# Part of du*B moved to TensorE, sums over states by transposes, convolutions on 32x32 tiles

## The chip, the cores and the metric

The kernel runs on one core of a Trainium2 chip. The metric is the device time of one execution in microseconds (us). The kernel before took 19,314.11 us (median of three runs, 19,313.31 to 19,316.24).

## The reference

Four layers follow one another on an image of 4 x 48 x 48 pixels with 192 channels, all in float32. Each of them contains selective scans over 2304 pixels (or, in the last layer, over rows of 48), with 16 states for each inner channel. The scan of the first layer, which the others share up to names:

```python
xz = u @ inW.T
xh, z = jnp.split(xz, 2, axis=-1)
xc = jax.nn.silu(_causal_conv(xh, cW, cB))
xdbl = xc @ xpW.T
dt = xdbl[..., :R]
Bm = xdbl[..., R:R + N]
Cm = xdbl[..., R + N:]
delta = jax.nn.softplus(dt @ dtW.T + dtB)
A = -jnp.exp(Alog)
def step(h, t):
    d_t, u_t, b_t, c_t = t
    h = jnp.exp(d_t[..., None] * A) * h + (d_t * u_t)[..., None] * b_t[:, None, :]
    return (h, jnp.sum(h * c_t[:, None, :], axis=-1))
...
y = jnp.swapaxes(ys, 0, 1) + xc * Dp
return y * jax.nn.silu(z) @ outW.T
```

The first layer runs four such blocks with 384 inner channels (along columns forward and backward, then along rows both ways, with a normalisation between) and a causal convolution of 3 taps. The second layer has a convolutional branch and four scan directions with 192 inner channels; the third has four scan directions without projections. The last layer runs four blocks with 384 inner channels and 4 taps on single rows and single columns (the state starts at zero in each), and then an MLP.

## The kernel before

**Jobs and groups.** The image is cut into six chunks of 384 pixels. A job is one chunk of one image in one scan direction; each of the four layers has 96 jobs. In the first and the last layer a job has 384 inner channels, as three blocks `i` of 128 partitions, and 16 states, as four groups `g` of NG = 4. So it has 12 groups. In the two layers between, the partitions hold two halves of the states of 64 channels (`parts = 2`), and a job has 6 groups. A group is a tile of 128 partitions by four states by 384 pixels (385 where the state is carried from chunk to chunk, with one column for the entering state).

**One group.** `decay` makes the four tiles exp(delta * A) on ScalarE, and with `i == 0` fetches B and C of the group's states, each row copied to all 128 partitions (`fetch`, one tile `bcb` of 2 x 4 x 384). `scan` does two VectorE instructions: the product of `du` (in PSUM) with B of the four states into the PSUM tile `inputs`, and one scan over the four states laid end to end. `weigh` multiplies h by C on GpSimd. `reduce` sums the four states on TensorE, each as a product with an identity, into the PSUM tile `y` of the block; `skip` puts D * x there first, by a diagonal matrix. When all four groups are in, `take` copies `y` to SBUF on ScalarE (`yt`) and `gate` multiplies it by silu(z) on GpSimd.

**One job.** `units` lists what a job needs before its groups: projections `inner`, depthwise convolutions `conv` (products with one diagonal 128x128 matrix per tap, then Silu on ScalarE), `bc` (B, C and the low-rank dt of the chunk, copied to SBUF as `bcd` and stored to DRAM as `bc`), `delta` (dt, Softplus), the gate's z, and the outputs of an earlier job. `drive` makes delta * x on GpSimd (`dus`), and `enter` copies it into the PSUM tile `du`. In the last layer a forward job and its backward twin share projections and z.

**The order.** `run_jobs` writes the order of every engine by hand, and TensorE, VectorE, GpSimd and ScalarE keep it. In turn t it issues: `scan` of group t; `decay` of group t + 2; `take` of a finished block; `weigh` of group t; then what the `Stream` of the next job's units has in this slot (0 to 11), its TensorE part before its ScalarE part, at most two units ahead, since the PSUM pool `ps` has two buffers; the side work of a normalisation, in some jobs; `gate` of an earlier block; `drive` of the block that begins at group t + 3; and `reduce` of group t - 1 (`behind` = 1). There are three buffers of decays, four of h in the last layer and three in the first, and five and four of `bcb`. All DMAs go through the queue of SyncE.

Of the kernel before, what the change touches and what calls it, by code (L numbers as in the profile page):

```python
# [14 lines left out]
ALU = mybir.AluOpType  # L15
# [11 lines left out]
NG = 4  # L27

# [30 lines left out]
class K:  # L59
# [3 lines left out]
    def __init__(self, tc, ctx):  # L63
        self.tc, self.nc = tc, tc.nc
        self.v, self.g, self.t = (
            InOrder(tc, e) for e in (tc.nc.vector, tc.nc.gpsimd, tc.nc.tensor)
        )
        self.count = 0
        self.last_act = None
        self.table = None  # L70
        self.const = ctx.enter_context(tc.tile_pool(name="const", bufs=1))
        self.ident = self.tile(self.const, [128, 128], "ident")
        make_identity(self.nc, self.ident)

# [163 lines left out]
class ScanPools:  # L238
# [6 lines left out]
    def __init__(self, k, ctx, parts, rows):  # L245
        pool = k.tc.tile_pool
        self.parts, self.rows = parts, rows
# [9 lines left out]
        self.y = ctx.enter_context(pool(name="y", bufs=2 if rows else 1, space=PSUM))  # L257
# [3 lines left out]
        inputs = k.tile(self.vec, [128, 1536 if rows else 2048], "inputs")  # L261
        self.b = inputs[:, : NG * W].rearrange("p (j l) -> p j l", l=W)
# [4 lines left out]
        self.n_decays = 0  # L267

# [40 lines left out]
class ScanJob:  # L309
# [12 lines left out]

    def __init__(self, k, pools, w, c0, rev, prev):
# [7 lines left out]
        self.du = {}  # L331

# [14 lines left out]
    def projections(self, xs, *slots):  # L347
# [5 lines left out]
        def bc(px):  # L353
# [4 lines left out]
            self.bc = k.dram([2 * N, W], "bc")  # L358
            nc.sync.dma_start(self.bc, self.bcd[: 2 * N, :])
# [21 lines left out]

    def fetch(self, g):
# [3 lines left out]
        self.bcb[g] = k.tile(pools.bcs, [128, 2, NG, pools.W], "bcb")  # L386
        self.fetched[g] = []
        for m in range(pools.parts):
            at = (m * pools.groups + g) * 2 * NG
            ins = k.nc.sync.dma_start(  # L390
                self.bcb[g][m * wide : (m + 1) * wide].rearrange("p s j l -> p (s j l)"),
                self.bc[at : at + 2 * NG, :].rearrange("r l -> (r l)").partition_broadcast(wide),
            )
            self.fetched[g].append(ins)

# [18 lines left out]
    def carry(self, i, g):  # L414

        if not self.pools.rows and self.prev is not None:
            at = self.entry
            ins = self.k.g.tensor_copy(
                self.bcb[g][:, 0, :, at : at + 1].squeeze(2),
                self.prev.state[:, i, g * NG : (g + 1) * NG],  # L420
# [8 lines left out]
    def enter(self, i):  # L429

        self.pools.turn(self.k, self.rev)
        self.pools.entered = self.k.copy(self.pools.du[:, self.tokens], self.du.pop(i))

    def scan(self, i, g):
# [6 lines left out]
        if pools.n_h >= pools.hbufs:  # L441
# [5 lines left out]
            b, du.unsqueeze(1).to_broadcast([128, NG, W]), self.bcb[g][:, 0, :, :], ALU.mult  # L447
# [3 lines left out]
        k.v.tensor_tensor_scan(  # L451
            h.rearrange("p j l -> p (j l)")[:, ::step],
            self.a.pop((i, g)).rearrange("p j l -> p (j l)")[:, ::step],
            b.rearrange("p j l -> p (j l)")[:, ::step],
            0.0,
            ALU.mult,
            ALU.add,
        )

    def weigh(self, i, g):  # L460
# [11 lines left out]
        ins = k.g.tensor_tensor(ht, ht, self.bcb[g][:, 1, :, self.tokens], ALU.mult)  # L472
        pools.weighed.append(ins)

    def reduce(self, i, g):
# [6 lines left out]
        h = self.h.pop((i, g))  # L482
        for j in range(NG):
# [63 lines left out]
class MambaJob(ScanJob):  # L547
# [50 lines left out]

    def units(self, last):
        k, w, two, halo = self.k, self.w, self.pools.two, self.w.taps - 1  # L600
# [13 lines left out]
        def conv(i, *slots):  # L614

            offs = [at + (halo - t) * (1 if self.rev else -1) for t in range(w.taps)]

            def act(ps):
                if i == 0:
                    self.xs = k.tile(two, [128, 3, CH], "xc")  # L620
                k.act(self.xs[:, i, :], ps, AF.Silu, bias=w.cb[:, i, :])

            return self.unit(
                slots,
                128,
                lambda ps: (
                    self.shaped(ps),
                    [(w.diag[:, i, t, :], self.part(i, off)) for t, off in enumerate(offs)],
                ),
                act,  # L630
            )
# [9 lines left out]
        if self.twin is not None:  # L641
# [3 lines left out]
            return [conv(0, 0, 0), conv(1, 1, 2), conv(2, 2, 2), bc, *deltas, *outputs]  # L645
# [6 lines left out]
            *(conv(i, min(2 + i, 3), 3) for i in range(3)),  # L652
# [10 lines left out]
    def skip(self, i):  # L663

        self.k.mmo(self.y[i], [(self.w.diagD[:, i, :], self.xs[:, i, :])], stop=False)

    def take(self, i):
        if i == 0:
            self.yt = self.k.tile(self.pools.one, [128, 3, CH], "yt", self.pools.yts)
        self.k.copy(self.yt[:, i, :], self.y[i])  # L670
# [115 lines left out]
def run_jobs(jobs, side=None):  # L786
# [4 lines left out]
    ahead, behind, taken, gated, driven = 2, 1, 2, 3, 3  # L791
# [20 lines left out]
    jobs[0].enter(0)  # L812
    for job, i, g in groups[:ahead]:
        job.decay(i, g)
    stream = Stream([])
    for t in range(len(groups) + gated + 1):
# [21 lines left out]
        if t < len(groups):  # L838
# [4 lines left out]
            job.weigh(i, g)  # L843
        stream.run(at if at < per - 1 else per)
        if t < len(groups):
# [12 lines left out]
        if 0 <= t - behind < len(groups):  # L858
            job, i, g = groups[t - behind]
            job.reduce(i, g)  # L860
    Stream(jobs[-1].outputs(*[(0, 0)] * 3)).run(per)
# [37 lines left out]
class MambaWeights(Weights):  # L899
    def __init__(self, k, pool, inT, xpT, dtT, vec, tag):  # L900
# [6 lines left out]
        self.diag = k.tile(pool, [128, 3, self.taps, 128], f"diag{tag}")  # L907

    def scaled(self, out, by):
        self.k.nc.vector.tensor_scalar(out, self.k.ident, by, None, ALU.mult)  # L910

    def diagonals(self, i):

        self.scaled(self.diagD[:, i, :], self.D[:, i, :])
        for t in range(self.taps):
            self.scaled(self.diag[:, i, t, :], self.vec[:, i, 19 + t : 20 + t])
# [13 lines left out]
class PairWeights(MambaWeights):  # L930
# [18 lines left out]
    def scaled(self, out, by):  # L949
        if not self.late:  # L950
            return super().scaled(out, by)
        self.k.act(out, self.k.ident, AF.Identity, scale=by)
# [933 lines left out]
```

## Time and profile before

| | |
|---|---|
| median of three runs | 19,314.11 us |
| profiled execution, its own time | 19,328.76 us |
| its span | 19,327.0 us |
| VectorE busy | 18,079.9 us (94%) |
| TensorE matmul busy, weight loads busy | 16,851.2 us (87%), 7,999.8 us (41%) |
| GpSimd busy | 14,748.4 us (76%) |
| ScalarE busy | 13,012.9 us (67%) |
| DMA, share of 16 engines | 41.1% |
| first layer, last layer | about 0 to 6,150 us, 12,836 to 18,890 us |

In the profile PE is TensorE, PEld its weight loads, DVE VectorE, ACT ScalarE, POOL GpSimd and SP SyncE. A group's line gives line, engine and operation, output and inputs by the names of the program's tiles, shapes, count, then the busy time in us and the mean of one in ns, then the engine's idle time before it with what ended it. Nearly all instructions have line 56, that of a helper which records the order, so they are told apart by tiles and shapes. A timeline's line gives start, length, engine, operation and count. A float32 product shows as two MATMULs with a weight load each.

### The profile page before, as it was taken

The numbers are of one execution on the slowest core, as the hardware profiler recorded it, in microseconds if no ns is written. First come the engines' busy times: TensorE is split into PE (matmuls) and PEld (weight loads), VectorE is DVE, ScalarE is ACT, GpSimd is POOL, SyncE is SP. The second block draws the span as 40 slices with busy tenths as digits, with TensorE's granted clock in tenths as the row PEclk, the third lists the DMA queues.
The fourth block names the chain that finished last, engine by engine and source line by source line (L and its number), as shares of the span: only waits on it lengthen the run. The fifth ranks groups of instructions, "written<-read, shape, count | busy, mean of one in ns | idle before, by whom it ended". The sixth has DMA issues, their size and how long they took to land.

```text
span 19327.0 us, 166155 instructions
## 1 busy us (share of the span) xinstructions
PE 16851.2 (87%) x49392; PEld 7999.8 (41%) x49392; DVE 18079.9 (94%) x7297; ACT 13012.9 (67%) x23158; POOL 14748.4 (76%) x10860
## 2 busy tenths in 40 slices
PE   8999999999998877787787778879999999999989
PEld 4544545444444322222222222234444444444444
DVE  9999999999998699999999999969999999999993
ACT  6766767666665467777777777766666666666663
POOL 7888888778886288888888888857777777777770
PEclk9999999999999878788887787889999999999999
DMA  3333333232332366666666666633322332333231
GB/s 114 118 112 115 122 110 127 104 117 106 117 117 90 91 142 141 151 149 152 151 150 146 141 151 148 140 110 110 107 106 104 107 112 105 109 110 112 103 107 47
DMA packets 500517, 2306.77 MB, mean 119 GB/s; under 512 B 76664, under 2 KB 334304, under 8 KB 347168
## 3 DMA queue, kind: packets, MB, share of 16 engines
q1 hardware_dynamic: 499616, 2296.14, 41.1%
q8 instruction: 396, 6.49, 0.1%
q14 instruction: 505, 4.14, 0.1%
HBM read 2103.60 MB, written 192.32 MB: 119 GB/s over the span
## 4 chain that ended last, share of the span: by engine, by line
DVE 47%; POOL 31%; PE 9%; issue 8%; ACT 3%; DMA 1%; POOLq 0%; SPq 0%; DVEq 0%; ACTq 0%
DVE h L56 30%; POOL h L56 24%; DVE inputs L56 16%; PE y L56 3%; PE ps L56 3%; POOL dus L56 2%; PE vps L128 2%; POOL state L56 1%; POOL yt L56 1%; ACT a L93 1%; PE mop L128 1%; POOL bcb L56 1%; PE mps L128 1%; DMA bcb<-bc 1%; POOL nx L56 1%
## 5 line engine op out<-in xcount | busy, mean ns | idle before, releaser
L56 POOL TENSOR_TENSOR h<-h,bcb 128x1536 f32<-128x1536 f32 x3456 | 11906.7, 3445 | 1599.4 <-DVE h L56 1137.0
L56 DVE TENSOR_TENSOR_SCAN h<-a,inputs 128x1540 f32<-128x1540 f32 (+1 forms) x3456 | 11606.4, 3358 | 145.0 <-DVE inputs L56 1.4
L93 ACT ACTIVATE a<-delta,A 128x384 f32<-128x384 f32 (+1 forms) x13824 | 7419.1, 602 | 2684.0 <-DVE h L56 2666.7
L56 PE MATMUL y<-h,ident 128*128 128x384 f32 x18432 | 6741.6, 514 | 440.9 <-POOL h L56 438.2
L56 DVE TENSOR_TENSOR inputs<-du,bcb 128x1540 f32<-128x1540 f32 (+1 forms) x3456 | 6112.5, 1769 | 419.0 <-ACT a L93 120.1
L56 PEld LDWEIGHTS y<-h,ident 128*128 128x128 f32 x18432 | 3614.9, 200 | 3410.5 <-POOL h L56 863.3
L56 PE MATMUL y<-h,sum 128*64 128x384 f32 x9216 | 2668.5, 643 | 746.0 <-POOL h L56 540.2
L56 POOL COPY state<-h 128x4 f32<-128x4 f32 x2304 | 431.5, 187 | 1950.4 <-DVE h L56 1912.0
L56 PEld LDWEIGHTS y<-h,sum 128*64 128x64 f32 x9216 | 853.6, 167 | 2175.2 <-issue 968.8
L56 PE MATMUL ps<-xh,diag 128*128 128x384 f32 x4032 | 1418.8, 491 | 171.2 <-ACT xc L93 171.0
L56 PE MATMUL ps<-bcd,dtT 12*128 12x384 f32 (+1 forms) x2304 | 1138.8, 608 | 453.0 <-ACT delta L93 449.7
L56 PE MATMUL ps<-u,inT 96*128 96x384 f32 x3456 | 1253.7, 493 | 162.2 <-ACT z L93 118.5
L56 PEld LDWEIGHTS ps<-xh,diag 128*128 128x128 f32 x4032 | 750.6, 189 | 765.9 <-ACT xc L93 259.3
L93 ACT ACT_TABLE_LOAD x794 | 1018.7, 1283 | 14.0
L90 ACT ACT_TABLE_LOAD x789 | 1012.3, 1283 | 14.2 <-PEq L1876 0.7
L56 PEld LDWEIGHTS ps<-u,inT 96*128 96x128 f32 x3456 | 650.0, 191 | 673.6 <-ACT z L93 194.8
L93 ACT ACTIVATE delta<-ps,vec 128x384 f32<-128x384 f32 x1152 | 632.2, 578 | 384.5 <-PE ps L56 379.1
L93 ACT ACTIVATE o<-ps 64x384 f32<-64x384 f32 (+1 forms) x864 | 409.2, 474 | 711.0 <-PE ps L56 711.0
L56 PEld LDWEIGHTS ps<-bcd,dtT 12*128 12x128 f32 (+1 forms) x2304 | 427.4, 213 | 1098.0 <-ACT delta L93 693.6
L56 PE MATMUL ps<-yt,outT 128*96 128x384 f32 x2304 | 789.8, 486 | 0.4 <-POOL yt L56 0.4
L93 ACT ACTIVATE du<-dus 128x384 f32<-128x384 f32 x1152 | 557.6, 484 | 141.1 <-DVE inputs L56 132.2
L56 PE MATMUL ps<-yc,sum 128*64 128x384 f32 x1152 | 643.6, 649 | 0.7 <-ACT yc L93 0.7
(133 smaller groups left out, 10570.8 us busy)
## 6 DMA issues: line engine op xcount, KB each, us to landing
bcb<-bc SPq DMA_DIRECT2D x384, 1540.0 KB
bcb<-bc SPq DMA_DIRECT2D x768, 770.0 KB
bcb<-bc SPq DMA_DIRECT2D x384, 1536.0 KB
y<-o SPq DMA_DIRECT2D x192, 288.0 KB
xs<-xi_wh SPq DMA_DIRECT2D x96, 288.0 KB
xs<-xi_hw SPq DMA_DIRECT2D x96, 288.0 KB
added<-y SPq DMA_DIRECT2D x96, 288.0 KB
xs<-x_wh SPq DMA_DIRECT2D x96, 288.0 KB
```

Source lines behind the costliest of these rows:

```text
L56: return lambda *a, **kw: self.tc.keep_in_program_order(op(*a, **kw))
L90: self.in_order(self.nc.scalar.preload_act_table_set(LOG_EXP))
L93: return self.in_order(self.nc.scalar.activation(out, in_, func, **kw))
L128: ins = (engine or self.nc.tensor).matmul(out, lhsT, rhs, start=start and i == 0, stop=stop and i == n - 1)
```

## The change

**du*B.** Of the four states of a group, VectorE keeps the product for `given` = 4 - `made`; TensorE makes the rest, `made` = 1 in the first layer, 2 in the last and none between. To have du on the contracted side, `turn` transposes `du` of a block on TensorE (three 128x128 transposes through `ps`, copied to SBUF by ScalarE as `duT`). B of a made state has to stand on the diagonal of a 128x128 matrix for each 128 pixels: `spread` stores these rows to DRAM as `be`, and copies them element by element from there onto the diagonals of images in DRAM that are zeroed once per layer (8 of them, two sets of four used in turn). `fetch` loads the diagonal matrices with a second DMA, into the same tile as B of the given states and C. `fill` then makes three products of 128 columns for each made state into the PSUM tile `fills`, which has one buffer. The scan of a group becomes two instructions, over the given states from `inputs` and over the made ones from `fills`; in the first layer the second scan starts from the carried state as its initial value.

**Sums.** With one part, `reduce` adds the four states to `y` by twelve 128x128 transposes that accumulate in PSUM, so `y` stands transposed (pixels on partitions). `skip` becomes three products with x as the stationary operand. `take` copies the transposed `y` to SBUF (`yT`), and the new `turn_back` transposes it back through `ps`, with another ScalarE copy to `yt`. `y` has one PSUM buffer in all layers (it had two in the last).

**Convolutions.** The diagonal matrices become strips of 32 columns. A unit makes two halves of 192 pixels, each by four 32x32 tiles per tap, so that eight products stand on eight different tiles; it holds both buffers of `ps`, and ScalarE applies Silu to each half. To make room for two halves at once, quarter r of a block goes to quarter (r + i) % 4; the weights are permuted on the host (`TURN`) to match.

**Order.** `behind` becomes 2 in the last layer; `take` and the gate follow it. All three convolution units of a forward job have slot 3. In turn t, `turn_back` comes before the stream, `turn` (for the block that begins at t + 2) after it, and `fill` of group t + 1 last, after `reduce`.

The core of the diff:

```diff
-        inputs = k.tile(self.vec, [128, 1536 if rows else 2048], "inputs")
-        self.b = inputs[:, : NG * W].rearrange("p (j l) -> p j l", l=W)
+        banks = -(-self.given * W // 512)
+        inputs = k.tile(self.vec, [128, banks * 512], "inputs")
+        self.b = inputs[:, : self.given * W].rearrange("p (j l) -> p j l", l=W)
+        self.fills = []
+        if made:
+            fills = k.tile(self.vec, [128, made * 512], "fills")
+            starts = (512 - CH, 512) if made == 2 else (0,)
+            self.fills = [fills[:, at : at + CH] for at in starts]
+            self.joined = fills[:, starts[0] : starts[0] + made * CH]
...
+            for n in range(2 * self.groups):
+                d = k.dram([128 * (self.line + 1)], "dg")
+                k.nc.sync.dma_start(d.rearrange("(t x) -> t x", x=self.line + 1), zeros)
+                self.diags.append(d)
...
+    def spread(self):
+        k, pools = self.k, self.pools
+        sync = k.nc.sync
+        n = N // NG * (pools.given + NG)
+        self.bc = k.dram([n, pools.W], "bc")
+        sync.dma_start(self.bc, self.bcd[:n, :])
+        if not pools.made:
+            return
+        be = k.dram([N // NG, pools.made, CH], "be")
+        sync.dma_start(be.rearrange("q e l -> (q e) l"), self.bcd[n : 2 * N, self.tokens])
...
+            for e in range(pools.made):
+                with k.nc.allow_non_contiguous_dma(reason="diagonal"):
+                    sync.dma_start(
+                        line[:, :, e, m, 0:1], be[q, e].rearrange("(b t v) -> t b v", t=128, v=1)
+                    )
...
+        if pools.made:
+            line = self.lines[g][: 128 * pools.line].rearrange("(t x) -> t x", t=128)
+            k.nc.sync.dma_start(t[:, n:], line)
...
+    def fill(self, i, g):
+        k, pools = self.k, self.pools
+        for b in range(3):
+            for e, out in enumerate(pools.fills):
+                for m in range(pools.parts):
+                    k.t.matmul(
+                        out[m * pools.wide : (m + 1) * pools.wide, b * 128 : (b + 1) * 128],
+                        self.duT[i][:, b, :],
+                        self.bcb[g][2][:, b, e, m, :],
+                        start=True,
+                        stop=True,
+                        skip_group_check=True,
+                    )
...
-            b, du.unsqueeze(1).to_broadcast([128, NG, W]), self.bcb[g][:, 0, :, :], ALU.mult
+            b, du.unsqueeze(1).to_broadcast([128, pools.given, W]), self.bcb[g][0], ALU.mult
...
+        n = pools.given
+        scan(flat(0, n), b.rearrange("p j l -> p (j l)"), 0.0)
+        if pools.made and pools.rows:
+            scan(flat(n, NG), pools.joined, 0.0)
+        elif pools.made:
+            for e, fill in enumerate(pools.fills):
+                j = g * NG + n + e
+                first = 0.0 if self.prev is None else self.prev.state[:, i, j : j + 1]
+                scan((v[:, n + e, self.tokens] for v in (h, a)), fill, first)
...
+        if parts == 1:
+            for j in range(NG):
+                ht = h[:, j, self.tokens]
+                for n in range(3):
+                    at = slice(n * 128, (n + 1) * 128)
+                    ins = k.t.matmul(
+                        self.y[i][:, at],
+                        ht[:, at],
+                        k.ident,
+                        start=False,
+                        stop=g == pools.groups - 1 and j == NG - 1,
+                        is_transpose=True,
+                        skip_group_check=True,
+                    )
+            pools.readers.append(ins)
+            return
...
+                for t, off in enumerate(offs):
+                    for r in range(4):
+                        at_r = slice(r * 32, (r + 1) * 32)
+                        for (i, n), ps in zip(both, made):
+                            c = (r + i) % 4
+                            k.t.matmul(
+                                self.shaped(ps[c * 32 : (c + 1) * 32]),
+                                w.diag[at_r, i, t, :],
+                                self.half(i, n, off)[at_r],
...
-            return [conv(0, 0, 0), conv(1, 1, 2), conv(2, 2, 2), bc, *deltas, *outputs]
+            return [conv(0, 0, 0), conv(1, 2, 2), conv(2, 2, 2), bc, *deltas, *outputs]
...
-            *(conv(i, min(2 + i, 3), 3) for i in range(3)),
+            *(conv(i, 3, 3) for i in range(3)),
...
     def take(self, i):
+        self.turned = self.k.tile(self.pools.one, [128, CH], "yT")
+        self.k.copy(self.turned, self.y.pop(i))
...
-    ahead, behind, taken, gated, driven = 2, 1, 2, 3, 3
+    behind = 2 if jobs[0].pools.rows else 1
+    ahead, taken, gated, driven = 2, behind + 1, behind + 2, 3
...
+        if back := at_group(t - gated, last_group):
+            back[0].turn_back(back[1])
         stream.run(at if at < per - 1 else per)
+        if soon := at_group(t + 2, 0):
+            soon[0].turn(soon[1])
...
             job.reduce(i, g)
+        if t + 1 < len(groups):
+            job, i, g = groups[t + 1]
+            job.fill(i, g)
```

## The prediction

> **What bounds the kernel now.** I read the page's busy line first, then the busy time by stage, the groups of instructions with shapes kept apart, and the timeline of single groups. The busy line and two long stretches, first the last layer (13,000 to 18,800 us), then the first (100 to 6,050 us):
>
> ```profile
> PE 16851.2 (87%) x49392; PEld 7999.8 (41%) x49392; DVE 18079.9 (94%) x7297; ACT 13012.9 (67%) x23158; POOL 14748.4 (76%) x10860
> 13000.00:18800.00 5800.00, 5316.37 (x15043) 2831.02 (x15042) 5703.64 (x2229) 3825.25 (x6591) 4449.57 (x2246) 0.95 0.30 108
> 100.00:6050.00 5950.00, 5540.20 (x15928) 2932.17 (x15928) 5731.22 (x2235) 4106.88 (x7222) 4897.10 (x4079) 0.97 0.32 114
> ```
>
> The columns of the stretches are length, busy PE, PEld, DVE, ACT, POOL, granted clock, DMA share, GB/s. DVE is 98% and 96% busy. The groups show what it does: one product and one scan for each of 3,456 groups of four states.
>
> ```profile
> L56 DVE TENSOR_TENSOR_SCAN h<-a,inputs 128x1540 f32<-128x1540 f32 x2304 | 7743.6, 3361 | 85.1
> L56 DVE TENSOR_TENSOR inputs<-du,bcb 128x1536 f32<-128x1536 f32 x1152 | 2034.5, 1766 | 76.2 <-ACT a L93 36.2 <-ACT du L93 0.3
> L56 POOL TENSOR_TENSOR h<-h,bcb 128x1536 f32<-128x1536 f32 x3456 | 11906.7, 3445 | 1599.4 <-DVE h L56 1137.0 <-issue 208.7 <-PE ps L56 55.7
> ```
>
> Next, a few groups in the timeline, DVE and then PE:
>
> ```profile
> 12883.35 1.77 DVE L56 TENSOR_TENSOR inputs<-du,bcb 128x1536 f32<-128x1536 f32 x1
> 12885.22 3.35 DVE L56 TENSOR_TENSOR_SCAN h<-a,inputs 128x1536 f32<-128x1536 f32 x1
> 12888.61 1.77 DVE L56 TENSOR_TENSOR inputs<-du,bcb 128x1536 f32<-128x1536 f32 x1
> ...
> 15000.72 2.74 PE L56 MATMUL y<-h,ident 128*128 128x384 f32 x8
> 15003.30 2.78 PE L56 MATMUL ps<-xh,diag 128*128 128x384 f32 x8
> 15005.92 0.81 PE L56 MATMUL y<-xc,diagD 128*128 128x384 f32 x2
> ...
> 8005.58 1.51 PE L56 MATMUL y<-h,sum 128*64 128x384 f32 x8 [1.65 <-POOL h L56]
> ```
>
> DVE repeats every 5.19 us, its 5.12 plus about 0.035 between instructions. A float32 product is two MATMULs; eight of 384 columns start within 2.58 us, so 0.323 each and 0.646 a product. The last line is eight of the same length on two column halves of the array: 1.51, not 2.74. Counting by job (12 groups): the last layer runs from DVE's first product at 12,872.8 to its last at 18,864.8, 62.5 us a job for 96 jobs; the first layer 63.7 (38.8 to about 6,150). PE really occupies 52 of 62.5: sums 12 x 2.58 = 31, convolutions 7.75, the other products about 13.5. So DVE sets the pace, and PE has only 16% to spare.
>
> **The skill.** "TensorE: Matmul & The Clock Gate", Terms, says that on this chip a transpose flag makes float32 four times faster, one pass instead of four; Part 3 says that matmuls on different tiles of the array run together. For the second the trace has the 1.51 us above; for the first it has no transpose at all. I go by both, and keep the doubt about the first for the range. Part 4 adds that transposes don't keep the clock up as matmuls do; no row here can show it, so it stands on the slow side.
>
> **DVE.** Two rows of products, 1536 elements in 1.766 us and 768 in 0.95 (the norm's ln_xm row of the timeline), give 1.06 ns an element and 0.14 fixed; the scan has twice that slope (8 ns more for 4 elements: 3361 against 3353) and, at 2.08 ns an element, 0.155 fixed.
> Last layer: product of 768 in 0.95, two scans of 768 in 1.75 each, three gaps of 0.035: a period of 4.56 for 5.19. First layer: product of 1155 in 1.37, scans of 1155 and 384 in 2.56 and 0.95, gaps: 4.98 for 5.20. If all else were hidden: 1152 x 0.63 + 1152 x 0.22 = 979 us. The layers between keep their DVE work.
>
> **TensorE's new prices.** No row has a transpose or a 128-column product. Loads of 128 columns follow each other after 0.11 (two for dtT take 0.29 in the prologue of the last layer, a single one 0.19), and a MATMUL of 128 columns is 0.323/3 = 0.108. A transpose that is one load and one pass thus costs 0.11, one that is done as a product 0.22; I take 0.11. A fill product is two pairs, 0.22.
> Per group of the last layer: sum 12 x 0.11 = 1.32 (was 2.58), fill 6 x 0.22 = 1.32. A convolution unit has 32 products, 64 MATMULs of 192 columns at 0.16: on eight tiles at once 1.3, with a tail 1.5; if only two run together, as the row of 1.51 shows for two tiles, 5.2. I take 1.5, so 4.5 a job for 7.75. Skips become nine products of 0.22 (2.0), turns to and fro 18 transposes (2.0); projections stay at 11.6. Sum 15.8 + 15.8 + 4.5 + 2.0 + 2.0 + 11.6 = 51.7 us a job: no less work than before, in a shorter period. In the first layer the fill is 0.66, a unit 1.2, PE about 47 of 60.
>
> **The new wait.** fills has one buffer. The fill of group t+1 may not start before the last scan of group t has ended (call it E), and must be done when DVE comes to its last scan: 0.95 + 1.75 + 0.1 = 2.8 us after E in the last layer, 1.37 + 2.56 + 0.07 = 4.0 in the first. Behind it in PE's queue stand the next group's convolutions, projections and sum, and ACT waits for these. PE may be 2.8 - 1.32 = 1.5 us late, then DVE stands. Places, by slot of the 12:
> (a) turn waits for drive, which POOL does after weigh: 3.45 + 1.0 + 0.1 = 4.55 after the E before, so at E itself. Then turn 0.33, skip 0.66, sum 1.32, fill 1.32: 3.63 against 2.8, 0.85 late, at slots 2 and 6 (and 10, where the gates' wait for ACT makes it 2.0 in forward jobs).
> (b) A convolution unit now holds both ps buffers, so units and ACT alternate. Four exponentials 2.1, a copy 0.45, the Silu table 1.28: ACT is ready 3.9 after the E before; a pair of halves takes 0.8. Forward jobs, slot 3: units end at 6.3 and 8.7, sum 10.0, fill 11.3, against 4.56 + 2.8 = 7.4: 3.9 late. Backward jobs, slot 2, two units: 6.3, buffers free 7.1, turn, skip, sum 9.4, fill 10.7: 3.3 late.
> (c) deltas 0.4 (both), outputs of 3.87 us at slots 7 and 9 and bc about 2.7 (backward).
> Together about 8.0 (forward) and 8.1 (backward), with 0.5 less where they overlap: 7.6 a job. Last layer: 12 x 4.56 + 7.6 = 62.3 for 62.5, so -20 us over 96 jobs. First layer: (a) fits in 4.0; (b) units end at 6.0 and 8.1, sum 9.4, fill 10.1, against 9.0: 1.1 late; with the 1.3 that the stage idles now, 12 x 4.98 + 2.4 = 62.2 for 63.7, -144 us.
>
> **Edits that I cost at nothing, and their cover.** ACT: 3.7 us a job more (halves 0.8, turned copies 2.9) on 41 of 62.5; its exponentials run two groups ahead. POOL: unchanged, 48 of 62. One y buffer for two: take is at 2.6, skip at 4.9 or later. bcb plus diagonal has the bytes of bcb before. SP issues 9 DMAs of spread and 4 loads of lines more per job: 384-element loads of vec take 0.4 to 0.6 us of SP each, 6 us of 62 in all, past bc and ahead of the next u. Diagonals: written at 2.2 (bc and be land) + 4 to 6, read 3 later, so about 13 us; first needed five groups, 23 us, later. If a 4-byte element took 0.1 us on its ring (24 elements x 8 = 19 us) it would just fit; beyond, rival three. Starts: 8 zero images of 0.39 MB (last layer) and 0.2 (first) ahead of the first loads at 150 GB/s are 31 us, partly beside weights, plus the longer first chain: +35 in all, 15 to 60.
>
> **Sum.** The profiled execution took 19,328.8 (its span 19,327.0). -144 - 20 + 35 = -129: 19,200. The median of the runs lies 15 lower, so 19,185; I say 19,190.
>
> **Rivals.**
> *DVE stays the bound.* PE's lateness overlaps more than I allow (loads pulled ahead over waits, units at 1.3): last layer 54.7 + 1.8 = 56.5, first 61.5; 96 x 6.0 + 96 x 2.2 - 35 = 752 less: 18,560. For it: PE's sum leaves 10 us of 62. Against: (a) and (b) are in the order of the queues.
> *PE doesn't fit (slower).* In the last layer, from about 0.12 us a transpose on, each further 0.01 adds 1.4 us a job of PE work with nowhere to go. At 0.16 (load and pass not overlapping: 0.11 + 0.05) PE has 60 us plus the 8 of its waits, 68: +5.5 x 96 = 530, first layer even: 19,850. At 0.22: 20,600. Two tiles at a time (unit 5.2) gives much the same as 0.22. A granted clock of 0.8, which the layers between have now, lies at 19,900. For it: PE's 52 of 62. Against: the page on transposes, and the eight overlapping MATMULs.
> *The diagonals come late.* At 0.2 us an element 38 us of ring time per job and a wait of some 10 us for it: 20,200. For it: nothing here writes 4 bytes to DRAM; against: 0.30 DMA share.
> That the change doesn't do what it says is no case: DVE's products shrink by their shape.
>
> **Chances.** Mine 0.40 (its own range 19,000 to 19,390), DVE bound 0.22, PE 0.32, diagonals 0.06. Under 0.2% (39 us) can't be told from no change in this kernel. Of mine 0.27 are faster, 0.08 same, 0.05 slower. So faster 0.49, same 0.08, slower 0.43. The range, 18,600 to 20,150, leaves out a tenth at each end: most of the best case below 18,600 and PE at 0.2 or more.
>
> **What would show it.** Right: products of 128x768 and 128x1155 at 0.95 and 1.37; scans of 768 at 1.75; PE rows of y with 128 columns, about 0.11 apart; DVE waiting before its second scan for PE fills, in the last layer some 7 us a job and in the first 1; turn waiting for POOL dus; convolutions waiting for ACT xc. Wrong: transposes 0.16 apart or in pairs; DVE at 98% again; a PE clock under 0.9; PE waiting for a DMA of the diagonal.

## The result and the profile after

The changed kernel takes 19,628.2 us (median of four runs, 19,608.3 to 19,675.3) against 19,315.2 before (four runs): a ratio of 1.0165, 95% interval 1.0146 to 1.0184. It is slower by 313 us. Its profiled execution took 19,608.3 us, 279.5 more than the one before.

By stage, from VectorE's first product to its last in the trace of either kernel (a job is twelve of the 1,151 periods between them):

| | before | after | difference |
|---|---|---|---|
| first layer | 6,135.8 us, 63.97 a job | 6,176.3 us, 64.39 a job | +40 |
| last layer | 5,992.0 us, 62.47 a job | 6,241.2 us, 65.07 a job | +249 |
| all else | | | -10 |

The busy line of the page after, and the two stretches that were shown of before (last layer, then first; length, busy PE, PEld, DVE, ACT, POOL, granted clock, DMA share, GB/s):

```profile
PE 16490.0 (84%) x113328; PEld 10674.8 (54%) x113328; DVE 16782.4 (86%) x9604; ACT 13503.5 (69%) x24886; POOL 14740.9 (75%) x10862
13000.00:18800.00 5800.00, 5126.90 (x49143) 4221.94 (x49143) 4634.39 (x3208) 3899.53 (x7129) 4260.38 (x2155) 0.96 0.34 105
100.00:6050.00 5950.00, 5116.41 (x41297) 3914.36 (x41295) 5313.58 (x3327) 4315.42 (x8001) 4861.42 (x4049) 0.93 0.35 114
```

VectorE shed 1,297 us of work, as it should. But in the last layer it is busy for 80% of the time where it was 98%. The groups, with shapes kept apart, say what it waits for (behind the count: busy us, mean ns | idle us just before, and what ended it):

```profile
L57 DVE TENSOR_TENSOR inputs<-du,bcb 128x768 f32<-128x768 f32 x1152 | 1108.0, 962 | 32.4 <-DMA dg<-be 32.4
L57 DVE TENSOR_TENSOR_SCAN h<-a,inputs 128x768 f32<-128x768 f32 x1152 | 2019.8, 1753 | 60.7 <-DVE inputs L57 1.4
L57 DVE TENSOR_TENSOR_SCAN h<-a,fills 128x768 f32<-128x768 f32 x1152 | 2003.7, 1739 | 1191.8 <-PE fills L57 1191.8
L57 DVE TENSOR_TENSOR_SCAN h<-a,state,fills 128x384 f32<-128x384 f32 x960 | 954.4, 994 | 437.4 <-PE fills L57 435.5
L57 DVE TENSOR_TENSOR_SCAN h<-a,fills 128x384 f32<-128x384 f32 x192 | 179.4, 934 | 88.0 <-PE fills L57 87.8
L57 PE MATMUL ps<-ident,dus 128*128 128x128 f32 x1728 | 330.3, 304 | 678.8 <-POOL dus L57 646.1 <-ACT xc L102 30.8
L57 PE MATMUL ps<-xh,diag 32*32 32x192 f32 x32256 | 947.2, 333 | 219.9 <-ACT xc L102 212.6 <-ACT xh L102 0.2 <-issue 0.2
```

What it lost again is the wait for `fills`: 1,191.8 us in the last layer, 12.4 a job, and 525.4 in the first, 5.5 a job. The last two lines are TensorE's own waits, in which the fills are stuck: `turn` waits for GpSimd's `dus`, convolutions wait for ScalarE's `xc`.

The timeline shows one such place, slots 1 to 4 of a backward job of the last layer; first DVE, then PE.

```profile
16220.20 0.96 DVE L57 TENSOR_TENSOR inputs<-du,bcb 128x768 f32<-128x768 f32 x1
16221.19 1.75 DVE L57 TENSOR_TENSOR_SCAN h<-a,inputs 128x768 f32<-128x768 f32 x1
16228.33 1.75 DVE L57 TENSOR_TENSOR_SCAN h<-a,fills 128x768 f32<-128x768 f32 x1 [5.38 <-PE fills L57]
16230.00 0.96 DVE L57 TENSOR_TENSOR inputs<-du,bcb 128x768 f32<-128x768 f32 x1
16231.00 1.75 DVE L57 TENSOR_TENSOR_SCAN h<-a,inputs 128x768 f32<-128x768 f32 x1
16238.39 1.75 DVE L57 TENSOR_TENSOR_SCAN h<-a,fills 128x768 f32<-128x768 f32 x1 [5.63 <-PE fills L57]
...
16215.15 1.48 PE L57 MATMUL y<-ident,h 128*128 128x128 f32 x12
16216.47 1.50 PE L57 MATMUL fills<-bcb,duT 128*128 128x128 f32 x12
16221.65 0.90 PE L57 MATMUL ps<-ident,dus 128*128 128x128 f32 x3 [3.68 <-POOL dus L57]
16222.34 1.49 PE L57 MATMUL y<-diagD,xc 128*128 128x128 f32 x6
16223.62 2.77 PE L57 MATMUL y<-ident,h 128*128 128x128 f32 x12
16226.18 2.11 PE L57 MATMUL fills<-bcb,duT 128*128 128x128 f32 x12
16228.13 0.49 PE L57 MATMUL ps<-ident,yT 128*128 128x128 f32 x3
16228.55 2.19 PE L57 MATMUL ps<-xh,diag 32*32 32x192 f32 x64
16231.29 1.85 PE L57 MATMUL ps<-xh,diag 32*32 32x192 f32 x64 [0.55 <-ACT xc L102]
16233.70 1.85 PE L57 MATMUL ps<-xh,diag 32*32 32x192 f32 x64 [0.55 <-ACT xc L102]
16235.48 1.53 PE L57 MATMUL y<-ident,h 128*128 128x128 f32 x12
```

TensorE stands at `turn` for 3.68 us. What follows takes longer than usual: the sum 2.77 us against 1.48 at the top, `skip` 1.49 against 0.83 elsewhere, the fill 2.11 against 1.50. The granted clock (the third figure from the end) says why:

```profile
16215.10:16217.90 2.80, 2.80 (x25) 2.62 (x23) 2.70 (x3) 2.55 (x6) 2.80 (x2) 1.00 0.17 59
16221.70:16223.60 1.90, 1.90 (x9) 1.90 (x10) 1.25 (x1) 1.02 (x3) 1.90 (x1) 0.50 0.00 0
16223.60:16226.10 2.50, 2.50 (x14) 2.50 (x13) 0.00 (x0) 1.88 (x4) 1.41 (x1) 0.50 0.00 0
16226.10:16228.10 2.00, 2.00 (x14) 2.00 (x13) 0.00 (x0) 0.00 (x0) 0.00 (x0) 0.66 0.00 0
```

TensorE works at half clock here until the fill is under way. Then come the three convolution units, 2.4 to 2.7 us from start to start, because each waits until ScalarE has emptied both `ps` buffers. Both fills are late, and VectorE stands 5.38 and 5.63 us.

"TensorE: Matmul & The Clock Gate", Part 1, in the Trainium skill says that the array falls to half clock after an idle window of about 3.4 us. The 3.68 us above agree. The traces also have half clock without such a wait (last section).

Half clock is only a part of the loss. The mean granted clock of the last layer is 0.96, and it was 0.95 in the same stretch before, so half clock is not new with this change; in the first layer it is 0.93 for 0.97. With drops to 0.50, a mean of 0.96 means about 8% of the time at half clock, some 5 us of the 65 of a job, and TensorE loses at most half of that. This is an estimate of 2.6 us a job, where VectorE waits 12.4.

As means over all jobs, VectorE's waits before the second scan stand at few slots (us; the lateness arises in the turn before). Backward jobs of the last layer: 3.2 at slot 3, 5.5 at 4, 2.5 at 7, 2.4 at 8, 1.6 at 11, together 15.2. Forward jobs: 3.0 at slot 3, 0.75 at 4, 1.1 at 6, 0.85 at 7, 2.3 at 8, 1.2 at 10, 0.3 at 11, together 9.6. First layer: 0.6 at slot 3, 3.0 at 4, 1.9 at 8.

### The profile page after: what moved, and what is told of

The parts are those of the page before. It is cut to its first block, busy times and chain, and to the rows that moved or that the text cites. A ratio compares the mean times of both kernels' runs of the same rounds, so it can differ in the third digit from the quotient of the medians.

```text
span 19606.5 us, 302357 instructions
## 1 busy us (share of the span) xinstructions
PE 16490.0 (84%) x113328; PEld 10674.8 (54%) x113328; DVE 16782.4 (86%) x9604; ACT 13503.5 (69%) x24886; POOL 14740.9 (75%) x10862
## 2 busy tenths in 40 slices
DMA packets 1075354, 2321.91 MB, mean 118 GB/s; under 512 B 550584, under 2 KB 858400, under 8 KB 921440
## 5 line engine op out<-in xcount | busy, mean ns | idle before, releaser
L57 DVE TENSOR_TENSOR_SCAN h<-a,inputs 128x1155 f32<-128x1155 f32 (+2 forms) x3456 | 8839.4, 2558 | 145.6 <-DVE inputs L57 1.4
L57 DVE TENSOR_TENSOR inputs<-du,bcb 128x1155 f32<-128x1155 f32 (+2 forms) x3456 | 4719.8, 1366 | 277.2 <-POOL bcb L57 94.4
L57 PE MATMUL y<-ident,h 128*128 128x128 f32 x27648 | 3799.6, 292 | 216.9 <-POOL h L57 214.1
L57 PEld LDWEIGHTS y<-ident,h 128*128 128x128 f32 x27648 | 3397.6, 152 | 713.1 <-POOL h L57 381.1
L57 DVE TENSOR_TENSOR_SCAN h<-a,fills 128x768 f32<-128x768 f32 (+1 forms) x1344 | 2183.1, 1624 | 1279.8 <-PE fills L57 1279.6
L57 PE MATMUL fills<-bcb,duT 128*128 128x128 f32 x20736 | 2875.6, 286 | 224.9 <-DVE h L57 181.6
L57 PEld LDWEIGHTS fills<-bcb,duT 128*128 128x128 f32 x20736 | 2649.4, 201 | 322.3 <-DVE h L57 258.8
L57 DVE TENSOR_TENSOR_SCAN h<-a,state,fills 128x384 f32<-128x384 f32 x960 | 954.4, 994 | 437.4 <-PE fills L57 435.5
L57 PE MATMUL ps<-xh,diag 32*32 32x192 f32 x32256 | 947.2, 333 | 219.9 <-ACT xc L102 212.6
L57 PEld LDWEIGHTS ps<-xh,diag 32*32 32x32 f32 x32256 | 616.3, 106 | 493.8 <-ACT xc L102 397.6
```

What stands on the lines that cost most here:

```text
L57: return lambda *a, **kw: self.tc.keep_in_program_order(op(*a, **kw))
```

## The experiments

The theory after this reading: the fill stands in TensorE's queue behind waits for other engines (GpSimd for `turn`, ScalarE for units that share two `ps` buffers), and half clock behind these waits makes them longer. The main rival: TensorE has too much work, and would be late in any order. Where one time is given, the kernel was executed once. The four executions of the changed kernel lie 67 us apart, so smaller differences between single ones rest on the waits in the traces. On the same chips the kernel before took 19,305.6 us beside the first three experiments and the first form of the fourth, 19,328.9 beside the late delta and the last two, and 19,314.6 (median of seven) beside the others.

**Drive one turn earlier.**

```diff
-    ahead, taken, gated, driven = 2, behind + 1, behind + 2, 3
+    ahead, taken, gated = 2, behind + 1, behind + 2
+    driven = 4 if jobs[0].pools.made else 3
```

> drive is issued one turn earlier in the first and the last layer (four turns ahead in place of three), so that GpSimd has dus ready when TensorE comes to turn; no work is added or removed. Theory (the fill stands in TensorE's queue behind waits for other engines): the waits of turn for dus (646 us in all) fall below 100, and VectorE's waits for fills at the slots after a turn shrink: in the last layer 3.2, 2.5 and 1.6 us at slots 3, 7, 11 of backward jobs, some 6 us of the 15, about 1 of the 9.5 in forward jobs, and 0.6 a job in the first layer. 96 x 3.5 + 96 x 0.6 = 390 us less: 19,220, between 19,100 and 19,350. Rival (TensorE simply has too much work): the waits stay where they are or move, within 60 us of 19,610. Rival (the convolutions that hold both ps buffers are the cause): less than 100 us gained.

Measured: 19,217.3 us, on the number, though in part by luck: the last layer gained 389 us for the 336 expected, the first 6 for 58, and the wait at slot 11 of backward jobs (1.6) stayed. The two rows of the groups view of this run:

```profile
L57 DVE TENSOR_TENSOR_SCAN h<-a,fills 128x768 f32<-128x768 f32 x1152 | 2000.9, 1737 | 818.6 <-PE fills L57 818.6
L57 PE MATMUL ps<-ident,dus 128*128 128x128 f32 x1728 | 287.1, 275 | 37.6 <-ACT xc L102 30.8 <-POOL dus L57 6.8
```

The wait for `dus` fell from 646 us to 7. The last layer came to 61.0 us a job from 65.1: the waits at slots 3 and 7 of its backward jobs are gone (3.2 and 2.5 to nothing). One small edit, no work removed, and the kernel is 0.5% faster than before. In the first layer nothing was won (64.3 a job): its wait at slot 3 went, and those at 4 and 8 stayed.

**Convolutions in slots of their own.**

```diff
-            return [conv(0, 0, 0), conv(1, 2, 2), conv(2, 2, 2), bc, *deltas, *outputs]
+            return [conv(0, 0, 0), conv(1, 1, 1), conv(2, 3, 3), bc, *deltas, *outputs]
...
-            *(conv(i, 3, 3) for i in range(3)),
+            *(conv(i, 3 + i, 3 + i) for i in range(3)),
```

> The convolution units get slots of their own: 3, 4, 5 in place of 3, 3, 3 for a forward job (and all jobs of the first layer), 0, 1, 3 in place of 0, 2, 2 for a backward one; bc and the outputs behind them move one or two slots later. Same products; ScalarE loads its Silu table two or one times more per job. Theory (TensorE waits for ScalarE inside a run of units): VectorE's wait at slot 4 of backward jobs of the last layer (5.5 us) and of all jobs of the first layer (3.0) falls to about 1, that at slot 3 of forward jobs from 3.0 to about 2: 96 x 2.7 + 96 x 2.2 = 470 us less, of which new small waits may take back 200: 19,140 to 19,350. Rival (too much work on TensorE): no change, 19,610 or more, since ScalarE has more to do. Rival (only the wait for drive matters): within 100 of 19,610.

Measured: 19,679.5 us, a miss: no better than the changed kernel. Two of the three waits aimed at went as expected, 5.5 to 0.8 at slot 4 of backward jobs and 3.0 to none at slot 4 of the first layer; that at slot 3 of forward jobs hardly moved (3.0 to 2.8). But bc and the outputs, pushed one or two slots on, met the deltas and made new ones: in the first layer 1.0, 2.2 and 3.5 at slots 6, 7 and 8, in the last 3.3 and 3.6 at 7 and 8. The last layer gained 131 us, the first lost 193. So these waits do come from the convolutions' place in the order, but removing them alone moved part of them elsewhere.

**No du\*B on TensorE.** All four states' products on VectorE again (`made` = 0 in both layers); sums, convolutions and order of after.

> VectorE makes du*B of all four states again in all layers (no turn, no fill, no diagonals, one scan a group); the sums by transposes, the convolutions on 32x32 tiles and the order of after stay. Theory: without fills nothing that TensorE is late with reaches VectorE, so the last layer goes back to 62.4 us a job and the first to about 63 (it was 63.9): 19,610 - 249 - 100 = 19,260, between 19,180 and 19,330. VectorE's waits for PE vanish. Rival (the convolutions on tiles or the turned sums slow the kernel by themselves, through ps or the single y buffer): the last layer stays above 63.5 us a job and the whole above 19,400.

Measured: 19,592.8 us, the rival's side: 64.1 us a job in the last layer and 65.2 in the first, more than before, with nothing to fill. In this order the turned sums and the tiles alone make the kernel as slow as the whole change does. The product's groups:

```profile
L57 DVE TENSOR_TENSOR inputs<-du,bcb 128x1540 f32<-128x1540 f32 x2304 | 4078.0, 1770 | 450.3 <-PE y L57 212.5 <-ACT a L102 44.1 <-POOL bcb L57 44.1
L57 DVE TENSOR_TENSOR inputs<-du,bcb 128x1536 f32<-128x1536 f32 x1152 | 2034.4, 1766 | 231.1 <-ACT du L102 88.8 <-PE y L57 71.4 <-ACT a L102 34.9
```

So I was wrong that without fills TensorE's lateness can't reach VectorE. It does through h: the sum (`y`) frees the buffer that a later scan needs, and the first layer has only three of them. Ahead of the product of slot 5 there VectorE stood 2.1 us, behind the convolution units. In the last layer more of the wait is for ScalarE's `du` (88.8 us) than for the sums (71.4); this was not followed further. The granted clock was 0.82 in the last layer and 0.86 in the first, lower than in after (0.96 and 0.93), and how much of the loss is the clock's was not tried here.

**TensorE kept busy ahead of turn**, in two forms: ten products more, written to the bank of `fills` or to the turn's own `ps` tile.

```diff
+        for _ in range(10):
+            k.t.matmul(ps[:, :128], k.ident, k.ident, start=True, stop=True, skip_group_check=True)
```

> Ten products of 128 columns (about 2.2 us of TensorE work, operands always ready, written to unused columns of the bank of fills) are put ahead of each turn, where TensorE waits for dus anyway: work is added, nothing else changes. Theory with the clock (after a wait of 3 us and more TensorE runs at half clock, and that doubles turn, skip, sum and fill behind it): the rows behind the wait run at full clock, the wait of VectorE at slot 3 of backward jobs falls from 3.2 us to below 1.5; gains and the 2.2 us where turn would not have waited about balance: 19,400 to 19,620. Waits without a clock effect: 19,600 to 19,750. Rival (TensorE has too much work): 3 x 2.2 us more in each of 192 jobs, 1270 us at most, above 20,200.

> Ten products of 128 columns (2.2 us of TensorE work) stand ahead of the three transposes of each turn, written to the turn's own ps tile, which the transposes then overwrite; unlike the products of the run before (to the bank of fills, where they waited for VectorE's scan) they wait for no more than turn does. Clock theory (TensorE falls to half clock when it waits for dus, and then turn, skip, sum and fill take twice their time): the rows behind the wait come back to 0.8, 1.5 and 1.5 us in place of 1.5, 2.8 and 2.1, VectorE's wait at slots 3 and 7 of backward jobs of the last layer falls from 3.2 and 2.5 us to about 1, other slots pay up to 1 us: 19,350 to 19,550. Waiting without a clock effect: 19,610 to 19,750. Too much work on TensorE: 6.6 us more in each of 192 jobs, up to 20,800.

Measured: 21,126.0 and 20,217.1 us, both misses. The first is no test of the clock: its products waited 722 us for VectorE's scans, although they write other columns of that tile than the scans read.

```profile
L57 PE MATMUL fills<-ident 128*128 128x128 f32 x11520 | 1652.8, 307 | 722.6 <-DVE h L57 722.3
```

The second is a test, and its outcome is mixed. Where `turn` had been waiting, the clock theory holds: the products (2.4 us) ran inside the wait and left 0.2 to 0.3 of it, the rows behind came back to 0.83, 1.47 and 1.50 us, and VectorE's waits fell from 3.2 to 2.0, 2.5 to 1.5 and, in the first layer, 0.6 to none. So by this test about 1.0 to 1.2 us of the first two waits were half clock. The other 1.5 to 2.0 go to the wait for GpSimd: with the earlier drive both waits vanished whole. Where turn had not waited, the 2.2 us came out nearly whole elsewhere (slot 11 of backward jobs 1.6 to 3.8, slot 3 of forward jobs 3.0 to 5.2). TensorE has no room there: the rival is not wrong, it is local.

**Convolutions of the last layer on 128x128 matrices again.**

```diff
-            return [conv(0, 0, 0), conv(1, 2, 2), conv(2, 2, 2), bc, *deltas, *outputs]
+            return [whole(0, 0, 0), whole(1, 2, 2), whole(2, 2, 2), bc, *deltas, *outputs]
```

> In the last layer alone the convolutions go back to 128x128 diagonal matrices, one block of 384 pixels and one ps buffer a unit, in the slots of after (u gets one buffer for two, to make room). TensorE has 7.75 us of convolutions a job for 4.5, 3.3 more. Theory (in after the unit and ScalarE take turns, so that a unit costs 2.4 us of the queue's time whatever its products take, 2.58 for a 128x128 unit): no change within 60 us of 19,610. Too much work on TensorE: 3.3 x 96 = 310 us more, 19,900. If tiles of 32x32 cost more than they save (clock, ps held): 150 us less or more, below 19,460.

(`whole` is a unit on 128x128 matrices; the forward jobs' units, the weights' layout and one buffer of `u` for two belong to the edit and are left out.) Measured: 19,736.8 us, 66.5 us a job for 65.1. Neither side's number: 128 us more than the profiled execution of after, of the 310 that TensorE's extra work comes to. The tiles save, but in this order less than half of the work that they save comes out as time. That the rest goes to the alternation with ScalarE is likely and not shown.

**The third delta one slot later**, on top of the earlier drive.

```diff
-                slots[1],
+                slots[1] if i < 2 or pools.parts == 2 else tuple(s + 1 for s in slots[1]),
```

> e1_drive_early, and the third delta unit of each job one slot later (8 for 7, 6 for 5), so that TensorE doesn't wait for ScalarE's Softplus with both ps buffers full; one more table load. It stands against e1_drive_early, 19,217. Theory (that wait of 1.0 to 1.5 us, and the half clock after products that use 12 rows, make the lateness of the deltas): the waits at slot 8 of backward jobs (2.5 us), slot 6 of forward jobs (1.2) and slot 8 of the first layer (1.7) go, of which new table loads at later slots take back up to half: 19,000 to 19,130. If the deltas are late by their own work alone, nothing is gained: 19,200 or more.

Measured: 19,165.2 us, 52 less than with the drive alone and 35 above the range (by stage, 67 less in the last layer and 13 more in the first). All three waits aimed at went to nothing (2.5, 1.2 and 1.7), so the deltas' lateness was the wait for ScalarE with what follows it, not their work. Which part of it was half clock behind them this run doesn't say. But slot 11 of backward jobs rose from 1.6 to 3.8, and slot 11 of the first layer from none to about 1: the cost moved to the turn with the gates.

**All in order at once (e8_order).** These edits together, with slots chosen by laying the durations of the trace into the queues:

```diff
-                slots[1],
+                slots[min(1 + i, len(slots) - 1)],
...
+            outputs = last.outputs(*((9, 10), (11, 11), (11, 11))) if last is not None else []
+            bc, deltas = self.projections(lambda: self.xs, (5, 6), *((7, 7), (7, 7), (8, 9)))
+            return [conv(0, 0, 0), conv(1, 3, 3), conv(2, 4, 4), bc, *deltas, *outputs]
+        if pools.rows:
+            bc, deltas = self.projections(lambda: self.xs, (5, 5), *((6, 6), (7, 8), (8, 8)))
+            return [
+                inner(0, 0, 0), inner(1, 1, 1), inner(2, 2, 2),
+                conv(0, 2, 2), conv(1, 4, 4), conv(2, 4, 4),
+                bc,
+                *deltas,
+                gate(0, 11, 11), gate(1, 11, 11), gate(2, 11, 11),
+            ]
...
+            inner(0, 0, 0), inner(1, 1, 1), inner(2, 1, 1),
+            conv(0, 1, 1), conv(1, 3, 3), conv(2, 4, 4),
+            bc, *outputs[:2], *deltas, *outputs[2:],
+            gate(0, 8, 9), gate(1, 11, 11), gate(2, 11, 11),
...
+    driven = 4 if jobs[0].pools.made else 3
...
-        stream.run(at if at < per - 1 else per)
         if soon := at_group(t + 2, 0):
             soon[0].turn(soon[1])
+        stream.run(at if at < per - 1 else per)
```

> The work of after, unit for unit, in another order: drive four turns ahead; turn ahead of the stream's units in its turn; convolutions in slots 0, 3, 4 (backward), 2, 4, 4 (forward) and 1, 3, 4 (first layer) so that ScalarE empties ps in between; bc, deltas, outputs and gates moved to slots of their own behind them; ScalarE loads more tables. Theory (waits in TensorE's queue and the half clock behind them are the loss): from the durations in the trace of after, laid into the new order, the last layer comes to 57 to 60 us a job (65.0 in after) and the first to 59 to 61 (64.3): 19,610 - 96 x 6.5 - 96 x 4.3 = 18,570, between 18,400 and 18,900. Too much work on TensorE: the last layer can't go below about 61, the whole stays above 19,100.

Measured: 18,531.2 us (four runs, 18,526.0 to 18,536.8), 0.9598 of the kernel before, interval 0.9583 to 0.9612. From the groups, and the stretch 13,000 to 18,000 us of the last layer:

```profile
L57 DVE TENSOR_TENSOR_SCAN h<-a,fills 128x768 f32<-128x768 f32 x1152 | 2001.7, 1738 | 440.8 <-PE fills L57 440.4
L57 DVE TENSOR_TENSOR_SCAN h<-a,state,fills 128x384 f32<-128x384 f32 x960 | 952.6, 992 | 95.5 <-PE fills L57 95.3
L57 PE MATMUL ps<-ident,dus 128*128 128x128 f32 x1728 | 283.6, 273 | 0.0
13000.00:18000.00 5000.00, 4811.91 (x48343) 3945.59 (x48342) 4535.96 (x3147) 4286.65 (x7345) 4185.71 (x2115) 1.00 0.38 119
```

The same 113,328 MATMULs as in after, 1,097 us less. The last layer takes 57.1 us a job and the first 61.1; waits for fills are 4.6 and 1.4 a job for 12.4 and 5.5. The granted clock is 1.00 there for 0.96, and TensorE is busy for 96% of the stretch. So its work was not what held the last layer at 65.1, though at 57 it is close to its limit. The edits were not tried one by one in this order, so the gain belongs to them together.

**The same with one made state in the last layer (e10_order_made1)**, with slots of its own.

```diff
-        pools = ScanPools(k, ctx, 1, True, 2)
+        pools = ScanPools(k, ctx, 1, True, 1)
```

> As e8_order, but in the last layer TensorE makes one of four states (three products of fill a group for six), with slots of its own: convolutions 0, 4, 5 and 1, 4, 5. VectorE's period there is 4.78 for 4.34 us, TensorE has 7.9 us a job less to do, and the fill has 4.0 us for 2.8. Theory: no wait is left in the last layer, 12 x 4.78 = 57.4, up to 58.5, as in e8_order or a little better: 18,350 to 18,650. If instead VectorE's own work decides once the order is mended, this is 12 x 0.44 x 96 = 500 us slower than e8_order.

Measured: 18,500.2 us (18,499.3 to 18,502.1), 0.9582 of before, interval 0.9566 to 0.9598; the intervals of the two overlap, though all its runs lie some 24 us or more under those of e8_order. In the last layer VectorE no longer waits for fills: 56.9 us a job, groups 4.72 to 4.79 us apart. One state made by TensorE does as well as two there: what the second would save VectorE, TensorE did not deliver in time in the order tried. This is the fastest version that was run.

**What the other parts bring in that order.** Convolutions of the last layer on 128x128 matrices, against e10_order_made1, and all of du\*B on VectorE, against e8_order:

> e10_order_made1 with the convolutions of the last layer on 128x128 diagonal matrices again (as in e7_conv128), in the same slots. TensorE does 3.3 us more a job, 47 us of 57. Theory (VectorE sets the pace there, no wait is left): within 50 us of 18,500. If TensorE has no room left: 100 to 300 us slower.

> e8_order with du*B of all four states on VectorE (no turn, no fill, no diagonals), so sums by transposes and convolutions on tiles alone, in the mended order. Theory: VectorE is back at 5.19 us a group, the last layer at 62.4 us a job, the first at 62.5 to 63.5: 18,531 + 96 x 5.3 + 96 x 2 = 19,230, between 19,120 and 19,310, a little below the kernel before at best: only the move of du*B pays. If the turned sums or the tiles gain something of their own: below 19,050.

Measured: 18,573.5 and 19,302.7 us. The first lies outside the 50 us expected and short of the rival's 100: the tiles are worth some 70 us (57.6 us a job for 56.9; a wait of 0.8 came up at slot 9 of forward jobs). Without du\*B on TensorE the last layer is back at 62.5 us a job, VectorE's bound, and the whole at the time of before: that move is worth some 770 us. Turned sums and tiles gain nothing without it; they pay by making room for it. The clock of the last layer fell to 0.84.

## Why the prediction was wrong

The prediction was 19,190 us, faster; the kernel is slower by 1.65%. The range held the time, but that was its width: the rival that lay nearest in it, dearer transposes, is not what happened.

**Prices of TensorE: right.** Twelve transposes start within 1.31 us, 0.109 each (0.11 taken); a fill of six products takes 1.34 from start to start (1.32). "TensorE: Matmul & The Clock Gate", Terms, calls the transpose mode four times faster for float32. In a stream here a transpose of 128 columns takes half of a product of 128 columns (0.109 against 0.223 us). Each has weight loads of its own, one for a transpose and two for a product, so this doesn't measure the pass alone. The convolution units alternate with ScalarE every 2.4 us in the last layer, as step (b) had it.

**VectorE's period: somewhat too long.** 4.32 to 4.39 us for 4.56, and 4.77 for 4.98. I took a gap of 0.035 us between instructions. The second scan and the next product start 0.08 before the one ahead has ended. That is 2.5 us a job in my favour.

**The failing step: the sum of lateness in "The new wait".** The places were right: the wait stands before the scan of `fills`, behind turn, convolutions, deltas and outputs. (A backward job's slots show the lateness of the stream that builds a forward job, one slot on.) The sizes were not:

| last layer, us a job | predicted | measured |
|---|---|---|
| stream builds a forward job: (a) turn, slots 2, 6, 10 | 0.85, 0.85, 2.0 | 3.2, 2.5, 1.6 |
| (b) convolutions | 3.9 | 5.5 |
| (c) deltas | 0.4 | 2.4 |
| sum | 8.0 | 15.2 |
| stream builds a backward job, all | 8.1 | 9.6 |
| mean | 7.6 | 12.4 |

Three things were missing in it. First, TensorE's clock: I took full clock behind every wait, and the rows behind `turn` took up to twice their prices. The experiment with the products in `ps` puts this at 1.0 to 1.2 us at each of two places of a backward job, and the estimate from the mean clock at no more than 2.6 us a job, so it is not all of the 4.8 us that were missing. Second, GpSimd: weigh and drive take 3.45 + 1.0 = 4.45 us in a period that I had made 4.56 and that is 4.35, so `dus` comes still later. Third, each place was worked out as if TensorE had come to it on time. Where the slots before are full (inner projections at slots 0 and 1), it hasn't. How the rest divides between the second and the third was not measured. Twelve periods of 4.35 and these waits make 52.2 + 12.4 = 64.6, of the 65.07 measured; predicted were 54.7 + 7.6.

**First layer.** Predicted 62.2 us a job with 1.1 of new wait, measured 64.4 with 5.5: convolutions 3.0 for 1.1, deltas 1.9 and turn 0.6 for nothing. Part (a) had been said to fit, and the deltas were not in the sum at all. The stage before took 63.97, not 63.7: its end had been read as about 6,150 us, and it is 6,174.6.

**Starts: overpriced.** VectorE's first product comes at 41.1 us for 38.8, and the gap ahead of the last layer shrank from 171 to 165 us; I had +35. The third rival is out as well: waits for `dg` are 32.4 us in all in the last layer's products, 0.3 a job.

**The rivals.** "PE doesn't fit" gave 19,850 and up by way of dearer transposes; they weren't dearer. "DVE stays the bound" failed in after, and is what the last layer of e10_order_made1 shows, with one made state and an order that the change didn't have.

In sum against the 279.5 us that the profiled executions differ by: -129 was predicted; the last layer is off by +269, the first by +184, the starts and the layers between by -45.

## What to carry to other kernels

A buffer that two engines hand over with no spare turns every wait in the producer's in-order queue into the consumer's wait: list what stands ahead of the handover, turn by turn, and let it start from where the turn before really ended. Price at half clock what follows a long wait of TensorE (3.68 us here; the waits of 0.55 us before the convolution units in that timeline left the clock at 1.00), and look up the granted clock where rows take longer than they should. Waits that are removed one at a time can move to the next full slot, as two of the experiments show, so judge an order as a whole: the same TensorE products took 19,628 us and 18,531.

## What was not expected of the hardware

- Half clock without a long wait. In the first layer with the earlier drive (timeline of that run), convolution units on 32x32 tiles ran at 2.48 us for 48 MATMULs after waits of 2.16 and 0.56 us; the same unit takes 1.2 to 1.5 elsewhere. The granted clock there is 0.50.

```profile
3222.99 2.48 PE L57 MATMUL ps<-xh,diag 32*32 32x192 f32 x48 [2.16 <-ACT xc L102]
3226.02 2.48 PE L57 MATMUL ps<-xh,diag 32*32 32x192 f32 x48 [0.56 <-ACT xc L102]
3228.43 2.05 PE L57 MATMUL y<-ident,h 128*128 128x128 f32 x12
```

  After delta products, which use 12 of the 128 rows, it needs no wait at all. In the run with products in `ps`, the sum and the fill behind them are slow although TensorE went from one to the other without a pause:

```profile
16540.96 2.49 PE L57 MATMUL ps<-bcd,dtT 12*128 12x384 f32 x6
16543.38 1.84 PE L57 MATMUL y<-ident,h 128*128 128x128 f32 x12
16545.02 2.77 PE L57 MATMUL fills<-bcb,duT 128*128 128x128 f32 x12
```

  The granted clock of that fill is 0.50. After has the same at 13,066 us: six delta products in 2.49 us, then a sum of 2.19 and a fill of 2.53 at 0.50. So small use of the array seems to count as idleness here; no run varies the rows alone.
- Less work, lower clock: 0.84 granted in the last layer with `made` = 0 in the mended order, 1.00 with `made` = 2. About a third of TensorE's work in the latter is transposes (162 of 0.109 us in 57 us a job), and they did not keep the clock down. Part 4 of the same page says that transposes don't count as busy in the same way; no run here has them without other products between.
- The MATMULs of a unit on 32x32 tiles start about 7 ns apart, eight in a row, before some 110 to 140 ns pass. A unit of 64 MATMULs lets the next instruction start after 1.5 us at best; with the waits for ScalarE the median is 2.4.
- Eight copies a job in the last layer and four in the first put 384 single elements of 4 bytes each onto diagonals in DRAM. Packets under 512 B rose from 76,664 to 550,584 and the DMA share only from 41.1% to 43.0%, and VectorE's products waited 32.4 us for these copies in all.
